# Third stage of a four-layer network: the order of all operations from one table of phases

## The chip, the cores and the metric

The kernel runs on one core of one Trainium2 chip. The metric is the device time of one execution in microseconds (us), as the median over runs of the same kernel. A core has a matrix engine (TensorE, PE in the profile; its weight loads are PEld), a vector engine (VectorE, DVE), a scalar engine (ScalarE, ACT), a general engine (GpSimd, POOL) and a sync engine whose queue (SP) issues transfers. Each engine takes its instructions in program order and waits for the others by semaphores.

## The reference, cut to what matters

The input x has shape (8192, 8, 16, 16). Four layers follow each other, each of the form x = x + layer(group norm(x)):

```
x = x + L0(gn(x))    # a tensor-train matrix of ranks 1, 8, 8, 1, plus a bias
x = x + L1(gn(x))    # 3x3 convolution, batch norm over all samples, ReLU
x = x + L2(gn(x))    # x and weights quantized to whole numbers by their global maxima,
                     # 3x3 convolution, divided by both scales, plus a bias
x = x + L3(gn(x))    # 3x3 convolution with edge padding, weights sign(w) * mean|w|, plus a bias
```

gn normalizes each sample over 4 groups of 2 channels. Two numbers need all samples before any sample can go on: the batch norm's moments (end of layer 1) and the maximum of |gn(x)| (start of layer 2's convolution). So the kernel has three stages; the third does layer 2's convolution, layer 3's group norm and layer 3's convolution.

## The kernel before

**Tiles.** The 8192 samples are 64 tiles of 128 samples. In the second and third stage a tile is an array of 128 partitions (8 channels x 16 rows) by 2048 columns (128 samples x 16 image columns), 1 MB. Thirteen tiles stay on the chip between the stages, the others are read from memory by `load3`, which is called at `rows2` for the tile four places on.

**What the third stage does with a tile.** It is cut into 26 operations, each a short function with a short name. In the order in which one tile goes through them:

- `rows2` (DVE), `spread2` (PE): the scale of each sample, from a small array spread over the partitions; it is written to columns 0 to 127 of the accumulator `ps_a` (read as `r2`).
- `v` (DVE, two halves, to int8), `q` (ACT, to bf16): quantized x. `bias` (ACT) adds layer 2's bias to the first half of x.
- `c2h0`, `c2h1` (PE, 6 products each, `pq` in the profile): layer 2's convolution of each half; `stz` (DVE) evicts the first half into x, `z1` (ACT) the second into a buffer that `add1` (POOL) adds to x.
- `sq` (ACT), `sums` (PE, 16 products, `s`), `small` (DVE, six short instructions), `pow` (POOL), `rows3` (DVE), `spread3` (PE, to `ps_r` and `ps_o`): layer 3's group statistics. `small` puts its transposed sums in columns 160 to 191 of `ps_a` (`st3`), and `rows3` reads them there.
- `t` (DVE, two halves): scaled x. `hi` (ACT): t rounded[...]; `lo` (POOL): the remainder; `edl` (ACT): the edge columns of lo (those of hi belong to `hi`). `c` (ACT) and `corr` (POOL): the offset of the group norm and the bias, added to x.
- `c3h0`, `c3h1` (PE, 12 products each, `pf`): layer 3's convolution of each half, six products with hi and six with lo; `out0`, `out1` (DVE) evict them into x. After the second, SP sends the tile to memory.

The four products of halves take turns in two accumulators of two banks each (`ps_c`): each one waits until the product before the last has been evicted.

**What sets the order.** Every engine's instructions keep the order in which the program names the operations. That order is the list `todo`. Its middle is written turn by turn from `TURN`, in which each operation has the offset of its tile: in a turn, `rows2` of tile i + 3 stands beside `out1` of tile i - 3, so a tile needs seven turns. The first 151 entries are replaced by `C_HEAD` and the last 130 by `C_TAIL`, two lists that name each operation with its tile (negative numbers count from the last tile: `spread2:-1` is tile 63). In `C_TAIL`, `small:-4` (tile 60) stands ahead of `spread2:-1`:

```
C_TAIL = """
...
bias:-2 t:-5 stz:-2 lo:-6 edl:-6 sums:-4 small:-4 bias:-3 corr:-6 c:-5 spread2:-1 c2h0:-3 stz:-3 pow:-4 c3h1:-7
...
```

For the last three tiles `c` is left out, and `corr` is done by DVE (two instructions) instead of POOL: see `offset3` and `add3`. Both convolution halves of layer 3 are one operation each, with the products of hi first, then those of lo: see `layer3`.

Of the kernel before, what the change touches and what calls it, by code (L numbers as in the profile page):

```python
# [8 lines left out]
F32 = mybir.dt.float32  # L9
# [4 lines left out]
ALU = mybir.AluOpType  # L14
# [4 lines left out]
P = 128  # L19
C, H, W = 8, 16, 16  # L20
# [5 lines left out]
QS = P // NQ  # L26
BANK = QS * W
# [17 lines left out]

C_HEAD = """
rows2:0 spread2:0 v:0 rows2:1 q:0 spread2:1 c2h1:0 rows2:2 bias:0 v:1 spread2:2 rows2:3 c2h0:0 v:2 z1:0 q:1
spread2:3 stz:0 add1:0 bias:1 c2h1:1 sq:0 c2h0:1 z1:1 v:3 sums:0 stz:1 small:0 q:2 add1:1 c2h0:2 c2h1:2 bias:2  # L50
rows2:4 pow:0 sq:1 rows2:5 rows3:0 z1:2 spread2:4 spread3:0 stz:2 t:0 q:3 sums:1 hi:0 c:0 small:1 v:4 add1:2 pow:1
bias:3 c2h0:3 spread2:5 rows3:1 sq:2 c2h1:3 spread3:1 stz:3 lo:0 sums:2 t:1 rows2:6 corr:0 edl:0 small:2 c:1 q:4
z1:3 hi:1 c3h0:0 pow:2 c3h1:0 v:5 add1:3 rows3:2 out0:0 bias:4 out1:0 lo:1 sq:3 q:5 spread3:2 spread2:6 c2h0:4 c:2
corr:1 edl:1 c2h1:4 rows2:7 z1:4 stz:4 t:2 hi:2 sums:3 c3h1:1 small:3 v:6 c3h0:1 out1:1 c2h1:5 pow:3 bias:5 rows3:3
spread3:3 lo:2 out0:1 q:6 spread2:7 rows2:8 z1:5 edl:2 v:7 c:3 add1:4 sq:4 c2h0:5 c3h0:2 bias:6 t:3 corr:2 stz:5
sums:4 c3h1:2 small:4 add1:5 hi:3 out0:2 c2h0:6 pow:4 rows3:4 sq:5 out1:2 spread2:8 stz:6 spread3:4 t:4 lo:3 c2h1:6
z1:6 corr:3 edl:3 sums:5 c:4 hi:4 small:5 pow:5 bias:7 v:8 q:7 add1:6
""".split()
C_TAIL = """
c2h1:-4 sq:-5 rows2:-2 rows3:-6 out1:-8 spread3:-6 rows2:-1 spread2:-2 c2h0:-4 v:-2 sums:-5 stz:-4 z1:-4 q:-3 t:-6  # L60
edl:-7 c3h0:-7 q:-2 small:-5 c2h1:-3 c:-6 out0:-7 c2h0:-2 hi:-6 add1:-4 sq:-4 pow:-5 rows3:-5 z1:-3 spread3:-5
bias:-2 t:-5 stz:-2 lo:-6 edl:-6 sums:-4 small:-4 bias:-3 corr:-6 c:-5 spread2:-1 c2h0:-3 stz:-3 pow:-4 c3h1:-7
hi:-5 out1:-7 c3h0:-6 rows3:-4 spread3:-4 add1:-3 c2h1:-2 sq:-3 lo:-5 z1:-2 out0:-6 v:-1 c3h1:-6 edl:-5 q:-1 add1:-2
sums:-3 t:-4 corr:-5 c:-4 c3h1:-5 out1:-6 small:-3 sq:-2 pow:-3 hi:-4 out1:-5 lo:-4 rows3:-3 bias:-1 sums:-2 c2h1:-1
small:-2 z1:-1 spread3:-3 edl:-4 c2h0:-1 c3h0:-5 c:-3 t:-3 stz:-1 add1:-1 pow:-2 corr:-3 rows3:-2 c3h1:-4 hi:-3
spread3:-2 sq:-1 out0:-5 c:-2 corr:-4 sums:-1 t:-2 lo:-3 hi:-2 small:-1 pow:-1 out1:-4 c3h0:-4 corr:-2 rows3:-1
out0:-4 edl:-3 c3h0:-3 spread3:-1 t:-1 lo:-2 c3h1:-3 out0:-3 edl:-2 out1:-3 hi:-1 c:-1 lo:-1 c3h0:-2 c3h1:-2 edl:-1
out0:-2 c3h0:-1 out1:-2 corr:-1 c3h1:-1 out0:-1 out1:-1
""".split()

# [6 lines left out]
def tile_net(ctx: ExitStack, tc: tile.TileContext, xb, xt_in, pack0, pack1, pack2, out):  # L79
    nc = tc.nc  # L80
    NT = xt_in.shape[0]

    pe, dve, act, pool = (InOrder(tc, e) for e in (nc.tensor, nc.vector, nc.scalar, nc.gpsimd))
# [78 lines left out]
    L = {}  # L162
# [127 lines left out]
    HALVES = [(0, P // 2), (P // 2, P)]  # L290

    def samples(t):
        return t.rearrange("p (b w) -> p b w", w=W)

    def over_w(stat, a, b):

        return stat[:, a:b].unsqueeze(2).to_broadcast([P, b - a, W])
# [25 lines left out]
    with first as s:  # L323
        small = s.enter_context(tc.tile_pool(name="small1", bufs=3))
# [5 lines left out]
        T = [dict() for _ in range(NT)]  # L330
# [267 lines left out]
        for n in range(NT * NQ):  # L598
            t, q = divmod(n, NQ)
# [62 lines left out]
        t = NT - 1  # L662
# [84 lines left out]
    small = ctx.enter_context(tc.tile_pool(name="small", bufs=4))  # L747
    kept = {}
    with tc.tile_pool(name="p2", bufs=2) as p2, tc.tile_pool(name="ps2", bufs=2, space=PSUM) as ps2:
        T = T2  # L750
# [8 lines left out]
        for k in range(3):  # L759
            nc.tensor.matmul(kps, L["gpad"].rearrange("p q j -> p (q j)"), L["band3"][:, k],  # L760
                             start=(k == 0), stop=(k == 2))
# [83 lines left out]
        for i in range(NT + 4):  # L845
# [4 lines left out]
            elif late:  # L850
                k, j = late.pop(0)
# [28 lines left out]
    with ExitStack() as s:  # L880
        wk = s.enter_context(tc.tile_pool(name="wk3", bufs=2))
        ps_c = s.enter_context(tc.tile_pool(name="ps_c3", bufs=2, space=PSUM))
# [4 lines left out]
        T = [dict() for _ in range(NT)]  # L887
# [4 lines left out]
        r2, r3, o3 = ps_a[:, 0:P], ps_r[:, 0:P], ps_o[:, 0:P]  # L892
# [11 lines left out]
        def halves(t):  # L904
            return t.rearrange("p (h n) -> p h n", h=2)
# [68 lines left out]
            stats_pow(T[i]["mv"])  # L974

        def offset3(i):
            if i >= NT - 3:
                return
            T[i]["c"] = small.tile([P, P], F32, name=f"c_{i}", tag="c")
            act.activation(T[i]["c"], o3, AF.Identity, bias=L["bias3"], scale=1.0)  # L980

# [20 lines left out]

        def add3(i):
            x = samples(T[i]["x"])
            if i >= NT - 3:
                for a, b in HALVES:
                    dve.scalar_tensor_tensor(x[:, a:b], over_w(o3, a, b), L["bias3"], x[:, a:b], ALU.add, ALU.add)
                return
            pool.tensor_tensor(x, x, over_w(T[i].pop("c"), 0, P), ALU.add)

        def edges3(i):
            edges(T[i]["lo"])

        def layer3(i, h):
            pc = ps_c.tile([P, 2, BANK], F32, name=f"pf_{i}_{h}", tag="pc")
            for m, t in enumerate(("hi", "lo")):
                for k in range(2):
                    q = 2 * h + k
                    tv = T[i][t][:, q * QS:(q + 1) * QS]
                    for n in range(3):  # L1020
                        pe.matmul(samples(pc[:, k]), L["sign3"][:, n], tv[:, :, n:n + W],
                                  start=(m == n == 0), stop=(m == 1 and n == 2))
            T[i]["pf", h] = pc

        def finish(i, h):
            x = halves(T[i]["x"])[:, h]
            pc = T[i].pop(("pf", h)).rearrange("p k n -> p (k n)")
            dve.scalar_tensor_tensor(x, pc, L["scale3"], x, ALU.mult, ALU.add)
            T[i]["done"] = T[i].get("done", 0) + 1
            if T[i]["done"] == 2:  # L1030
                nc.sync.dma_start(out[order[i]], T[i]["x"])
                T[i].clear()

        OPS = {"rows2": rows2, "spread2": spread2, "v": scale2, "q": round2, "bias": bias2,
               "c2h0": lambda i: layer2(i, 0), "stz": first2, "c2h1": lambda i: layer2(i, 1), "z1": second2, "add1": add2,
               "sq": square3, "sums": sums3, "small": stats3, "pow": pow3, "rows3": rows3, "spread3": spread3, "c": offset3,
               "t": scale3, "hi": high3, "lo": low3, "corr": add3, "edl": edges3,
               "c3h0": lambda i: layer3(i, 0), "out0": lambda i: finish(i, 0),
               "c3h1": lambda i: layer3(i, 1), "out1": lambda i: finish(i, 1)}
        TURN = [("rows2", 3), ("rows3", -1), ("out1", -3), ("sq", 0), ("c2h0", 1), ("stz", 1), ("spread2", 3), ("spread3", -1),  # L1040
                ("c", -1), ("c2h1", 1), ("z1", 1), ("add1", 1), ("v", 3), ("sums", 0), ("small", 0), ("pow", 0), ("t", -1),
                ("edl", -2), ("q", 2), ("hi", -1), ("bias", 2), ("lo", -1), ("corr", -1), ("c3h0", -2), ("out0", -2),
                ("c3h1", -2)]
        todo = [(op, i + k) for i in range(-3, NT + 4) for op, k in TURN if 0 <= i + k < NT]
        if len(todo) >= len(C_HEAD) + len(C_TAIL):
            head, tail = ([(op, int(i) + n) for op, i in (c.split(":") for c in l)] for l, n in ((C_HEAD, 0), (C_TAIL, NT)))
            todo = head + todo[len(head):len(todo) - len(tail)] + tail
        for i in range(AHEAD):
            load3(i)
        for op, i in todo:  # L1050
# [72 lines left out]
```

## Time and profile before

| what | us |
|---|---|
| median of 3 runs | 3834.26 (3833.98 to 3834.51) |
| span of the profiled execution | 3831.54 |
| time around the span, against the median | 2.7 |
| third stage: first DVE operation, end of last eviction | 3064.64, 3826.39 |
| PE busy over the span | 3606.5 (94%) |
| DVE | 3406.9 (89%) |
| POOL | 3040.9 (79%) |
| ACT | 2513.1 (66%) |
| groups of the third stage, one each: `v`, `t`, per half | 1.21 |
| `lo`, `corr`, `add1`, `pow` on POOL | 4.27, 3.69, 2.42, 1.02 |
| `hi`, `q`, `sq`, `z1`, `bias` on ACT | 1.93, 1.90, 1.90, 1.21, 1.15 |
| `stz`, `out0`, `out1` on DVE | 1.28, 1.26, 1.26 |

No time of the profiled execution beyond its span is recorded; 3831.54 is set beside the median, and the runs differ among themselves by 0.5. The page's busy shares are means over three stages of different make: the third is the last fifth of the span. In it all engines work on different tiles at once, so what counts is which engine is never idle, and who waits for whom where it is. Since a helper records every operation, all of them carry the same line (L43), and groups are told apart by the names of their tiles: x is `xs`, `u`, `xk`, `ys` or `bs`, t is `sq` or `xh`.

### The profile page before, as it was taken

The page shows a single profiled execution, that of the slowest core. Times are in us where ns is not written, and L with a number is a line of the kernel's source. Part 1 is how long each engine was busy: PE and PEld are TensorE (multiplying, and loading weights), DVE is VectorE, ACT ScalarE, POOL GpSimd, SP SyncE. Part 2 cuts the span into 40 slices and gives each one's busy share as a digit, 9 for nine tenths or more (in the row PEclk, how much of TensorE's full clock was granted, in tenths as well). Part 3 has the DMA queues.
Part 4 walks back from the last instruction along what each step waited for, and adds up shares of the span by engine and source line. Part 5 has one row for each costly group of instructions (what it writes and reads, how often), then busy time and mean ns, then how long its engine had stood idle before and what let it go on. Part 6 is the DMA issues. An engine that isn't in the chain of part 4 may idle for free. (4 is left out here: it accounts for less than half of the span.)

```text
span 3831.5 us, 52833 instructions
## 1 busy us (share of the span) xinstructions
PE 3606.5 (94%) x16326; PEld 2127.6 (56%) x16326; DVE 3406.9 (89%) x6319; ACT 2513.1 (66%) x2673; POOL 3040.9 (79%) x3101
## 2 busy tenths in 40 slices
PE   8999999999999999999999999997655599999998
PEld 4666666666666666666666666662211155555555
DVE  8988888888888888888888888877998889999997
ACT  5666666666666666666666666665665477777775
POOL 4877778777777787777777877766887779999997
PEclk9999999999999999999999999998776699999999
DMA  5787787888877878788788788757999724444432
GB/s 212 255 268 258 258 266 251 270 253 262 270 256 258 267 250 271 253 262 267 258 261 266 250 271 252 258 187 281 422 425 425 301 110 176 187 185 178 185 145 99
DMA packets 210809, 960.93 MB, mean 251 GB/s; under 512 B 44896, under 2 KB 45152, under 8 KB 110048
## 3 DMA queue, kind: packets, MB, share of 16 engines
q1 hardware_dynamic: 173808, 692.22, 48.7%
q0 software_dynamic: 36288, 264.26, 23.4%
q8 instruction: 131, 2.15, 0.2%
q14 instruction: 150, 1.23, 0.1%
q10 hardware_dynamic: 432, 1.08, 0.1%
HBM read 578.84 MB, written 378.54 MB: 250 GB/s over the span
## 5 line engine op out<-in xcount | busy, mean ns | idle before, releaser
L43 PE MATMUL po<-u,core 128*128 128x512 f32 (+1 forms) x4112 | 1844.7, 591 | 0.0
L43 ACT COPY u<-pu 128x2048 f32<-128x2048 f32 x512 | 956.7, 1868 | 511.9 <-PE pu L43 511.8
L43 PEld LDWEIGHTS po<-u,core 128*128 128x128 f32 x4112 | 744.7, 190 | 737.1 <-issue 736.1
L43 PE MATMUL pu<-core2r,xl 128*128 128x256 f32 x4032 | 678.5, 310 | 4.5 <-ACT u L43 3.6
L43 PEld LDWEIGHTS pu<-core2r,xl 128*128 128x128 f32 x4032 | 527.9, 189 | 127.8 <-issue 123.0
L43 POOL TENSOR_TENSOR bs<-bs,xh 128x512 fp32r<-128x512 f32 (+1 forms) x253 | 325.6, 1287 | 201.0 <-ACT xh L43 200.9
L43 POOL TENSOR_TENSOR v<-e 128x128 f32<-128x128 f32 x750 | 397.9, 542 | 0.0
L43 DVE TENSOR_TENSOR xs<-po,xs 128x512 f32<-128x512 f32 x256 | 177.0, 692 | 217.5 <-PE po L43 217.5
L43 ACT ACTIVATE m<-pm,b 128x128 f32<-128x128 f32 x250 | 92.0, 368 | 395.5 <-PE pm L43 395.5
L43 PEld LDWEIGHTS pm<-v,fast 128*128 128x128 f32 x2000 | 262.5, 191 | 119.7 <-issue 106.2
L43 POOL TENSOR_TENSOR e<-x1n,x 128x512 f32<-128x512 f32 x250 | 306.2, 1225 | 23.9 <-ACT x L43 16.4
L43 DVE TENSOR_TENSOR bs<-bs,stat 128x1024 f32<-128x1024 f32 x252 | 290.8, 1217 | 2.1
L43 POOL TENSOR_TENSOR xs<-xs,w 128x2048 f32<-128x2048 f32 x64 | 291.5, 4554 | 0.6 <-DMA xs<-in_xt 0.6
L43 PE MATMUL pm<-v,fast 128*128 128x128 f32 x2000 | 263.6, 275 | 0.0
L43 ACT ACTIVATE x<-x1n 128x512 f32<-128x512 f32 x500 | 247.1, 545 | 7.6 <-DVE x1n L43 7.6
L43 POOL TENSOR_TENSOR mv<-mv,mhalf 128x4 f32<-128x4 f32 x127 | 130.8, 1030 | 138.1 <-DVE mv L43 138.1
L43 PE MATMUL pf<-hi,sign 128*128 128x512 f32 x768 | 227.7, 434 | 0.5 <-DVE xs L43 0.5
L43 POOL DMA_DIRECT2D xl<-limb_d x252 | 150.0, 595 | 96.9 <-ACT x L43 29.1
L43 PE MATMUL pf<-lo,sign 128*128 128x512 f32 x768 | 219.4, 423 | 0.0
L43 POOL TENSOR_TENSOR v<-r 128x128 f32<-128x128 f32 x500 | 215.9, 448 | 0.0
L43 ACT ACTIVATE sq<-xs 128x2048 f32<-128x2048 f32 x103 | 196.8, 1911 | 4.7 <-POOL xs L43 4.6
L43 PE MATMUL gb<-rows_c,sel 128*128 128x128 f32 x128 | 40.3, 409 | 167.3 <-DVE rows_c L43 167.3
(310 smaller groups left out, 7202.4 us busy)
## 6 DMA issues: line engine op xcount, KB each, us to landing
xl<-limb_d POOLq DMA_DIRECT2D x252, 1024.0 KB, 7.4
x_d<-xs SPq DMA_DIRECT2D x76, 1024.0 KB, 8.4
xs<-in_xt SPq DMA_DIRECT2D x64, 1024.0 KB, 7.5
bs<-in_xb SPq DMA_DIRECT2D x63, 1024.0 KB, 5.7
limb_d<-xh SPq DMA_DIRECT2D x1008, 64.0 KB, 4.3
limb_d<-bs SPq DMA_DIRECT2D x1008, 64.0 KB, 5.2
y_d<-ys SPq DMA_DIRECT2D x60, 1024.0 KB, 8.0
u<-x_d SPq DMA_DIRECT2D x34, 1024.0 KB, 5.9
```

Source lines behind the costliest of these rows:

```text
L43: return self.tc.keep_in_program_order(op(*args, **kwargs))
```

## The change

The two lists and `TURN` go. In their place stands a table that gives each operation a phase, and a period; all operations of all tiles are sorted by period times tile plus phase, from the first to the last, with nothing special at the ends. The phases are only keys of the sort: no instruction waits for a time. Each half of layer 3's convolution is named as two operations, a (hi) and b (lo), which have phases of their own; a takes the accumulator. The exceptions of `offset3` and `add3` for the last three tiles are removed. Up to the third stage the program is the same, instruction by instruction.

```diff
-C_HEAD = """
-rows2:0 spread2:0 v:0 rows2:1 q:0 spread2:1 c2h1:0 rows2:2 bias:0 v:1 spread2:2 rows2:3 c2h0:0 v:2 z1:0 q:1
...
-C_TAIL = """
...
+PERIOD = 11.539
+PHASE = {"rows2": 0, "spread2": 0.01, "v": 5.1, "q": 10.2, "bias": 10.4, "c2h1": 11.6, "z1": 13.1, "c2h0": 16.1, "add1": 17.1,
+         "stz": 23.1, "sq": 24, "sums": 31.8, "small": 34.7, "pow": 37.3, "rows3": 42.7, "spread3": 45.3, "t": 46.3,
+         "hi": 49.9, "c": 51.2, "lo": 51.9, "corr": 58.8, "edl": 60.3, "c3h0a": 60.4, "c3h0b": 61.3, "out0": 66.8,
+         "c3h1a": 69.3, "c3h1b": 69.4, "out1": 69.41}
...
         def offset3(i):
-            if i >= NT - 3:
-                return
             T[i]["c"] = small.tile([P, P], F32, name=f"c_{i}", tag="c")
...
         def add3(i):
             x = samples(T[i]["x"])
-            if i >= NT - 3:
-                for a, b in HALVES:
-                    dve.scalar_tensor_tensor(x[:, a:b], over_w(o3, a, b), L["bias3"], x[:, a:b], ALU.add, ALU.add)
-                return
             pool.tensor_tensor(x, x, over_w(T[i].pop("c"), 0, P), ALU.add)
...
-        def layer3(i, h):
-            pc = ps_c.tile([P, 2, BANK], F32, name=f"pf_{i}_{h}", tag="pc")
-            for m, t in enumerate(("hi", "lo")):
-                for k in range(2):
...
+        def layer3(i, h, m):
+            if m == 0:
+                T[i]["pf", h] = ps_c.tile([P, 2, BANK], F32, name=f"pf_{i}_{h}", tag="pc")
+            pc, t = T[i]["pf", h], T[i]["hi" if m == 0 else "lo"]
+            for k in range(2):
...
-        TURN = [("rows2", 3), ("rows3", -1), ("out1", -3), ("sq", 0), ("c2h0", 1), ("stz", 1), ("spread2", 3), ("spread3", -1),
-                ("c", -1), ("c2h1", 1), ("z1", 1), ("add1", 1), ("v", 3), ("sums", 0), ("small", 0), ("pow", 0), ("t", -1),
-                ("edl", -2), ("q", 2), ("hi", -1), ("bias", 2), ("lo", -1), ("corr", -1), ("c3h0", -2), ("out0", -2),
-                ("c3h1", -2)]
-        todo = [(op, i + k) for i in range(-3, NT + 4) for op, k in TURN if 0 <= i + k < NT]
...
+        todo = [(op, i) for _, op, i in sorted((PERIOD * i + at, op, i) for op, at in PHASE.items() for i in range(NT))]
```

Sorted, the steady turn of the new order reads, with the tile of each operation counted from the newest (0), engine by engine:

| engine | before | after |
|---|---|---|
| PE | c2h0 -2, spread2 0, spread3 -4, c2h1 -2, sums -3, c3h0 -5, c3h1 -5 | spread2 0, c2h1 -1, c3h1 -6, c3h0 -5, c2h0 -1, sums -2, spread3 -3 |
| DVE | rows2 0, rows3 -4, out1 -6, stz -2, v 0, small -3, t -4, out0 -5 | rows2 0, stz -2, small -3, t -4, out1 -6, v 0, rows3 -3, out0 -5 |
| ACT | sq -3, c -4, z1 -2, edl -5, q -1, hi -4, bias -1 | sq -2, z1 -1, edl -5, hi -4, c -4, q 0, bias 0 |
| POOL | add1 -2, pow -3, lo -4, corr -4 | corr -5, pow -3, add1 -1, lo -4 |

The order of PE in the table of before is that of one turn as the program names it; the chain of a turn may be begun at any of its entries.

More of the change, by code (lines that the diff above doesn't have):

```diff
@@ L44, in __getattr__ @@
         return call
-C_HEAD = """
-rows2:0 spread2:0 v:0 rows2:1 q:0 spread2:1 c2h1:0 rows2:2 bias:0 v:1 spread2:2 rows2:3 c2h0:0 v:2 z1:0 q:1
[L50 to L58, printed above, removed]
-C_TAIL = """
-c2h1:-4 sq:-5 rows2:-2 rows3:-6 out1:-8 spread3:-6 rows2:-1 spread2:-2 c2h0:-4 v:-2 sums:-5 stz:-4 z1:-4 q:-3 t:-6
@@ L61 @@
[L61 to L69, printed above, removed]
+PERIOD = 11.539
[3 more added lines that the diff above has]
+         "c3h1a": 69.3, "c3h1b": 69.4, "out1": 69.41}
@@ L1012, in edges3 @@
             edges(T[i]["lo"])
-        def layer3(i, h):
-            pc = ps_c.tile([P, 2, BANK], F32, name=f"pf_{i}_{h}", tag="pc")
-            for m, t in enumerate(("hi", "lo")):
-                for k in range(2):
[L1018 to L1023, printed above, removed]
+        def layer3(i, h, m):
[3 more added lines that the diff above has]
+            for k in range(2):
+                q = 2 * h + k
+                tv = t[:, q * QS:(q + 1) * QS]
+                for n in range(3):
+                    pe.matmul(samples(pc[:, k]), L["sign3"][:, n], tv[:, :, n:n + W],
+                              start=(m == n == 0), stop=(m == 1 and n == 2))
         def finish(i, h):
@@ L1037, in tile_net @@
                "t": scale3, "hi": high3, "lo": low3, "corr": add3, "edl": edges3,
-               "c3h0": lambda i: layer3(i, 0), "out0": lambda i: finish(i, 0),
-               "c3h1": lambda i: layer3(i, 1), "out1": lambda i: finish(i, 1)}
-        TURN = [("rows2", 3), ("rows3", -1), ("out1", -3), ("sq", 0), ("c2h0", 1), ("stz", 1), ("spread2", 3), ("spread3", -1),
-                ("c", -1), ("c2h1", 1), ("z1", 1), ("add1", 1), ("v", 3), ("sums", 0), ("small", 0), ("pow", 0), ("t", -1),
-                ("edl", -2), ("q", 2), ("hi", -1), ("bias", 2), ("lo", -1), ("corr", -1), ("c3h0", -2), ("out0", -2),
-                ("c3h1", -2)]
-        todo = [(op, i + k) for i in range(-3, NT + 4) for op, k in TURN if 0 <= i + k < NT]
-        if len(todo) >= len(C_HEAD) + len(C_TAIL):
-            head, tail = ([(op, int(i) + n) for op, i in (c.split(":") for c in l)] for l, n in ((C_HEAD, 0), (C_TAIL, NT)))
-            todo = head + todo[len(head):len(todo) - len(tail)] + tail
+               "c3h0a": lambda i: layer3(i, 0, 0), "c3h0b": lambda i: layer3(i, 0, 1), "out0": lambda i: finish(i, 0),
+               "c3h1a": lambda i: layer3(i, 1, 0), "c3h1b": lambda i: layer3(i, 1, 1), "out1": lambda i: finish(i, 1)}
+        todo = [(op, i) for _, op, i in sorted((PERIOD * i + at, op, i) for op, at in PHASE.items() for i in range(NT))]
         for i in range(AHEAD):
```

## The prediction

> **What bounds the kernel now.** The change begins where the third stage begins, so I read that stage alone. First the table of stretches: the steady middle (first row) and the end.
>
> ```profile
> core 0: us, PE busy (x) PEld busy (x) DVE busy (x) ACT busy (x) POOL busy (x), PEclk, DMA share, GB/s
> 3400.00:3500.00 100.00, 100.00 (x500) 59.08 (x499) 93.27 (x165) 77.47 (x69) 97.51 (x36) 1.00 0.47 181
> ...
> 3760.00:3780.00 20.00, 16.14 (x75) 9.34 (x73) 12.49 (x26) 11.98 (x12) 17.42 (x7) 0.91 0.13 52
> 3780.00:3800.00 20.00, 20.00 (x104) 11.78 (x106) 18.00 (x33) 15.01 (x13) 18.34 (x8) 1.00 0.13 54
> ```
>
> In the middle TensorE (PE) is never idle, but POOL (97.5%) and DVE (93%) have little to spare; near 3770 PE has idled and its clock dropped. Then the chain of waits, which in the middle is PE alone:
>
> ```profile
> 3398.32 6.42 PE pf L43 x24
> ...
> 3744.71 6.42 PE pf L43 x24
> ```
>
> Thirty turns in 346.39 us: **11.546 us a turn**, one tile entering and one leaving. Then the timeline of PE, one steady turn from layer 2's products (pq) to the next turn's:
>
> ```profile
> 3404.57 1.47 PE L43 MATMUL pq<-q,band 128*128 128x512 bf16 x6
> 3405.88 0.39 PE L43 MATMUL ps_a<-rows_d,sel 128*128 128x128 f32 x2
> 3406.10 0.39 PE L43 MATMUL ps_r<-rows_e,sel 128*128 128x128 f32 x2
> ...
> 3409.79 1.82 PE L43 MATMUL pf<-hi,sign 128*128 128x512 f32 x6
> 3411.45 1.71 PE L43 MATMUL pf<-lo,sign 128*128 128x512 f32 x6
> 3413.00 1.72 PE L43 MATMUL pf<-hi,sign 128*128 128x512 f32 x6
> 3414.57 1.71 PE L43 MATMUL pf<-lo,sign 128*128 128x512 f32 x6
> ```
>
> Starts follow each other without a hole, so the turn is the sum of the starts' distances. Last, the waits and the timeline at the end:
>
> ```profile
> PE ps_a L43 <- DVE mv L43: 3.0, 1, 3.0
> PE pq L43 <- DVE bs L43: 0.8, 1, 0.8
> PE pf L43 <- DVE xs L43: 0.5, 2, 0.3
> ...
> POOL lo L43 <- ACT hi L43: 6.0, 3, 3.6
> ```
>
> ```profile
> 3764.45 1.04 PE L43 MATMUL s<-sq,wsum 128*32 128x512 f32 x8
> 3768.51 0.80 PE L43 MATMUL ps_a<-rows_d,sel 128*128 128x128 f32 x2 [3.02 <-DVE mv L43]
> 3769.10 2.72 PE L43 MATMUL pq<-q,band 128*128 128x512 bf16 x6
> ```
>
> PE waited 3.0 us for DVE, and the next six pq products took 2.72 us instead of 1.47.
>
> **The whole stage as an account of PE.** From DVE's first operation (3064.64) to the end of the last eviction (3826.39) are 761.75 us; 64 turns of work are 738.9. The other 22.9: waits in the head 10.2 (distances of starts beyond the usual ones: 0.7, 3.2, 1.1, 0.8, 1.2, 0.6, 2.6, 0.1), slow clock in the head about 4.5, the tail 6.8 (waits 1.0, 3.1, 0.45 and 0.33; slow clock 1.9), and 1.5 for the last product's end and its eviction. That adds to 23.0. A new order can change only the turn, the head and the tail.
>
> [...]spread2 writes columns 0 to 127 of ps_a, small reads columns 160 on, and PE still waited for the last read (mv).[...]
>
> **Part 1, the two groups.** In the table c3h0a and c3h0b (and c3h1a and c3h1b) have no other PE operation between their places, for any tile; the order of PE has high and low of a half next to each other everywhere. The accumulator is taken at the same place. Cost and gain: nothing.
>
> **Part 2, the steady turn.** No operation is added or dropped. PE's order per turn was c2h0, spread2, spread3, c2h1, sums, c3h0, c3h1; it becomes c2h1, c3h1 (older tile), c3h0, c2h0, sums, spread3, spread2. So two joins go (pq to spread; sums to pf) and two come (sums to spread; pq to pf). Sums to pf delays the first group: 3409.79 to 3411.45 is 1.66, a group inside 1.56, so 0.10 goes. Sums to a spread with no wait isn't in the trace; a spread after a wait is: 3076.47 to the following pq at 3076.80 is 0.33 against 0.22, so 0.11 comes. If that were hidden it would be 0[...]. Pq to pf is in the head: 3117.78 to 3120.62 is 2.84, against 1.31 + 1.56 = 2.87. The turn becomes 11.546 - 0.01, with bounds -0.13 and +0.10; over some 58 turns **-0.6 us** (-7.5 to +6).
>
> Will PE still never wait? I walked one turn with the measured durations (v and t 2.34 each, evictions 1.2 to 1.3, small 1.46, rows3 0.8; ACT hi 1.93, sq 1.90, z1 1.21, q 1.90; POOL lo 4.27, corr 3.69, add1 2.42, pow 1.02). The inputs that come closest: spread2 after rows2, 0.6 us early; c3h1 after stz frees its accumulator, 1.0; c3h0 after z1 frees the other, 1.0; c2h1 after q, 1.3; c2h0 after out1, 1.5; spread3 after rows3, 1.7; low products after edl, 2.1. (The second, from spread3 at 0: spread2 at 0.55, c2h1 at 0.78, so c3h1 at 2.1; stz, behind out0 and rows2 on DVE, ended at 1.0.) DVE, with 10.8 us of work, now idles 0.8 before out1, which stands behind t and waits for PE; v and rows3 queue behind it, and q on ACT waits for v: that is in the 1.3. POOL needs 4.23 + 3.65 + 2.37 + 1.02 = 11.27 from start to start; its waits (lo for hi, add1 for z1) fill the other 0.27. PE covers all this.
>
> Transfers: the tile's output leaves SP after out1, the same six turns after rows2 as now, and the load into its buffer 4 us later (out at 3406.15, load at 3410.18), landing in 6 to 9 us; it is read seven turns, 81 us, after. SP has no other queue here, POOL issues none: no cost.
>
> **Part 3, the head.** The table fills one tile per turn, the old list let layer 2 run ahead and put c3h0:0 and c3h1:0 side by side. Out1:0 comes some 6 us later, but that is not a loss: PE does other tiles meanwhile. Its waits, walked with the same durations: 0.6 and 3.0 (rows2:0, rows2:1 behind v:0 on DVE) and 0.9 (q:0), as now; 1.8, 0.9, 0.4 and 1.4 for q:1 to q:4, and 1.6 for rows3:1: **10.6 against 10.2**. One of them in full, from the stage's first operation: v:1 runs on DVE from 5.1 to 7.5; ACT takes z1:0 first (8.0 to 9.2, behind c2h1:0 at half clock) and then q:1 (9.1 to 11.0); PE is through with c2h0:0 and spread2:2 at 9.3, so c2h1:1 waits from 9.3 to 11.1, the 1.8. The slow clock I take as equal; it is 1 us either way. Part 3: +0.4 (-2 to +3).
>
> **Part 4, the tail.** The old list moved spread2:63 behind small:60 on ps_a; small:60 stood on DVE behind t:58 (3763.45, 2.35) and stz:61 (3765.72, 1.28), and ended at 3768.45. In the table spread2:63 keeps its steady place, 0.6 us behind rows2:63, and c2h0:62 no longer waits for out0. So the waits 1.0 + 3.1 + 0.45 + 0.33 and the 1.9 of slow clock go: 6.8. What is late next: when no new tiles enter, PE's turn shrinks to spread3 plus pf, 6.7 us, and POOL's lo + corr to 7.9. Corr of the last three tiles returns from DVE (2.47 each) to POOL (3.69), with c on ACT (0.36). POOL had idled 6.0 us before lo in the tail, so only corr:62, between lo:62 and lo:63, delays: PE, some 3 us behind, waits 0.4 us for edl:63 and 0.3 for rows3:63. Part 4: **-6.8 + 0.7 = -6.1** (-8 to -2).
>
> **Sum.** -0.6 + 0.4 - 6.1 = -6.3. The walk as a whole, laid against the trace of before, was 0.35 us short there; its own difference is -6.6, and -7 with the shorter turn; I take -6.7. The profiled span 3831.54 becomes 3824.8. The median 3834.26 is 2.7 above that span: 3827.6 us. 0.2%, about what a measurement of this kernel can tell from no change, is 7.7 us, down to 3826.6: the forecast lies just short of it.
>
> **The rivals.**
> A, faster: the first spread after sums is hidden. Then 0.11 x 58 = 6.4 more go: 3821.2. For it: weights of pf are loaded under the product before. Against: the same load after sums showed 0.10.
> B, no gain: the head costs what the tail gives, the 6 us of out1:0 surviving to the end: 3834. For it: POOL, at 97.5%, cannot catch up a late start quickly. Against: PE's waits, not out1:0, make the account.
> C, slower: POOL becomes the bound. Its 11.27 is 0.27 under PE's turn. If lo waits for hi and add1 for z1 one after the other, 0.5 us in all, the turn is 11.8: 60 x 0.25 - 6 = +9, 3843. It is slower by over 0.2% from 11.78 on. For it: add1 now stands between pow and lo, and z1 behind sq on ACT. Against: the walk has 0.31 of such waits, with 2 us between lo and the product that needs it.
> That the groups change nothing is Part 1, not a rival.
>
> **Numbers.** Main case 0.62 (3825 to 3831), A 0.18, B 0.13, C 0.07. A third of the main case lies beyond 3826.6, which with A makes faster 0.38; same 0.55 from the rest of it and B; slower 0.07. The range 3822.5 to 3832 leaves out C, the far part of A and the upper half of B.
>
> **What would show it.** Steady PE chain 11.53 to 11.55 a turn; out1:0 about 47 us after the stage's first operation; no wait of ps_a for mv, clock 1.00 from 3740 on; the last out1 near 3819.7. Wrong if the turn is over 11.6 with PE waiting for lo or q, or if the tail has a PE wait over 2 us.

## The result, and the profile after

| what | before | after |
|---|---|---|
| median, us (11 runs each) | 3832.91 (3831.44 to 3834.51) | 3824.30 (3822.28 to 3825.91) |
| ratio, 95% interval | | 0.9977 (0.9968 to 0.9986) |
| span of the profiled execution | 3831.54 | 3822.81 |
| third stage, first DVE operation to end of last eviction | 761.75 | 752.57 |
| steady turn | 11.546 | 11.473 |

The change takes 8.6 us off, 0.23%; the forecast was that it takes off 6.7. All of it is in the third stage: that stage is 9.18 us shorter and starts 0.4 us later in the profiled execution.

The table of stretches of the kernel after (columns as before): the steady middle first, then the end.

```profile
core 0: us, PE busy (x) PEld busy (x) DVE busy (x) ACT busy (x) POOL busy (x), PEclk, DMA share, GB/s
3400.00:3500.00 100.00, 99.53 (x502) 58.35 (x510) 92.26 (x170) 79.25 (x71) 98.36 (x35) 1.00 0.49 188
3760.00:3780.00 20.00, 19.95 (x102) 12.31 (x94) 17.52 (x34) 16.59 (x16) 19.81 (x9) 1.00 0.15 63
3780.00:3800.00 20.00, 19.64 (x99) 11.72 (x99) 15.59 (x30) 8.38 (x9) 18.17 (x7) 1.00 0.32 131
```

From 3760 to 3780 PE is busy for 19.95 us instead of 16.14, and its clock is 1.00 instead of 0.91. The shares of the middle look like those of before, although the turn there is shorter: a busy share doesn't show that. The chain of waits does (start, duration, what):

```profile
3384.47 6.15 PE pf L43 x24
...
3728.66 6.15 PE pf L43 x24
```

Thirty turns in 344.19 us: 11.473 a turn. In PE's timeline of one turn the starts tell where it went:

```profile
3486.27 1.46 PE L43 MATMUL pq<-q,band 128*128 128x512 bf16 x6
3487.37 1.90 PE L43 MATMUL pf<-hi,sign 128*128 128x512 f32 x6
3489.11 1.70 PE L43 MATMUL pf<-lo,sign 128*128 128x512 f32 x6
3490.64 1.70 PE L43 MATMUL pf<-hi,sign 128*128 128x512 f32 x6
3492.17 1.70 PE L43 MATMUL pf<-lo,sign 128*128 128x512 f32 x6
3493.71 1.47 PE L43 MATMUL pq<-q,band 128*128 128x512 bf16 x5
```

The last three groups of six start 1.53, 1.53 and 1.54 us apart; before, they were 1.55, 1.57 and (from 3414.57 to the next product) 1.55 apart. All 24 products are closer together. Instruction by instruction, the mean distance of starts inside such a row of 24 is 0.2558 us here and 0.2590 before. I call these the **256 pace** and the **259 pace**.

The waits of PE in the tail, from 3740 on, are down to two small ones (total us, count, longest; counted as distances of starts beyond the usual ones, as in the account below, they come to 0.51 and 0.47):

```profile
PE pf L43 <- ACT lo L43: 0.3, 1, 0.3
PE ps_r L43 <- DVE rows_e L43: 0.3, 1, 0.3
```

The account of the stage, made as for the kernel before (waits are distances of starts beyond the usual ones; slow clock in the head is what is left over, with the few rows of 24 at the ends that have the 259 pace):

| us | before | after |
|---|---|---|
| 64 turns | 738.9 | 734.3 |
| waits in the head | 10.2 | 10.1 |
| slow clock in the head, and rest | 4.5 | 5.7 |
| waits in the tail | 4.9 | 1.0 |
| slow clock in the tail | 1.9 | 0 |
| end of the last product and its eviction | 1.5 | 1.5 |
| sum | 761.9 | 752.6 |

So in this execution the tail brought 5.8 us, the turn 4.6, and the head took 1.1.

### The profile page after: what moved, and what is told of

Same layout as the page of the kernel before. It is cut to its first block, busy times and chain, and to the rows that moved or that the text cites. A ratio compares the mean times of both kernels' runs of the same rounds, so it can differ in the third digit from the quotient of the medians.

```text
span 3822.8 us, 52777 instructions
## 1 busy us (share of the span) xinstructions
PE 3598.8 (94%) x16264; PEld 2127.1 (56%) x16326; DVE 3386.0 (89%) x6313; ACT 2518.2 (66%) x2676; POOL 3048.8 (80%) x3104
## 4 chain that ended last, share of the span: by engine, by line
PE 85%; DVE 6%; DMA 4%; issue 2%; POOL 1%; ACT 1%; POOLq 0%; SPq 0%; DVEq 0%; ACTq 0%
PE po L43 45%; PE pu L43 12%; PE pf L43 10%; PE pm L43 6%; PE pq L43 4%; PE s L43 3%; PE pc L43 3%; DVE top L43 3%; PE ps_r L43 1%; DMA ys<-x_d 1%; DMA x_d<-u 1%; DMA x_d<-ys 1%; DMA u<-x_d 1%; DMA x_d<-xs 1%; DMA sq<-y_d 1%
```

## The experiments

Two questions. Do head, turn and tail have the shares of this account? And why are layer 3's products closer together: what stands ahead of them on PE, or what other engines do beside them?

**The head alone.**

```diff
+            table = [(op, i) for _, op, i in sorted((PERIOD * i + at, op, i) for op, at in PHASE.items() for i in range(NT))]
+            first = table[:255]
+            todo = first + [o for o in todo if o not in first]
```

> The kernel before with the first 255 operations taken from the table and the rest in the old order (layer 3's halves unsplit, the exception for the last three tiles kept). It measures the head by itself. As predicted (Part 3): +0.4 us against before, and some 0.6 us where the two orders meet (two waits of layer 2's products by the measured durations), so +1.0, bounds -1.5 to +3.5. By the account of the trace after, in which the head has about 1.1 us more of waits and slow clock, less some six turns of 0.07 us: +1.3. A head that costs all of its late start (rival B): +6.

Measured: 3834.33 us (13 runs), 1.0003 of before (0.9995 to 1.0011), which is +1.2 with an interval from -1.9 to +4.2. From PE's first spread to the last eviction the profiled execution has 760.94 us, before 761.09. The table's head costs about nothing, although out1:0 comes 6 us later; that the account has 1.1 for it is one execution's figure. In the kernel after, profiled a second time, the eviction of the first half of tile 10 began 0.95 us sooner (153.08 us after the first spread, not 154.03), and that stage was 1.0 shorter. The order is the same; what differs is that PE ran at half clock for one stretch of 3.41 us in the head, and in the first execution for 6.83. Rival B, in which that delay lives on to the end, is out.

**Head and turns from the table, the tail old.**

```diff
-            first = table[:255]
+            first = table[:-264]
```

> The kernel before with all but the last 264 operations taken from the table, and these last ones in the old order. Head and steady turns are the table's, the tail is the old one. Against head_only it differs in some 43 steady turns. Prediction (turn shorter by 0.01): 0.4 us below head_only, no gain against before. Rival, the turn gives near half of what the change brings (0.073 a turn as in the trace after): 3.1 us below head_only, some 2 us below before. If so, what is missing to the change, about 6 to 7 us, is the tail.

Measured: 3830.14 us (13 runs), 0.9993 of before (0.9985 to 1.0001), 4.2 us below the run with the new head alone; the expectation from the measured turn was 3.1, from the prediction 0.4. The turn is 11.473. By the profiled executions, which differ by 4.0 us in the stage, the rest lies in the clock: PE waits here as long as before for the last read of ps_a, but the clock stays at 1.00. Timeline; then the two stretches of 3.41 us that hold the wait, and for comparison those of the kernel before:

```profile
3766.53 0.49 PE L43 MATMUL ps_a<-rows_d,sel 128*128 128x128 f32 x2 [3.01 <-DVE mv L43]
3766.85 1.46 PE L43 MATMUL pq<-q,band 128*128 128x512 bf16 x6
```

```profile
3761.61:3765.02 3.41, 1.91 (x17) 0.40 (x16) 3.41 (x4) 2.88 (x4) 3.41 (x2) 1.00 0.00 0
3765.02:3768.43 3.41, 1.91 (x10) 1.21 (x11) 1.32 (x7) 1.04 (x2) 3.41 (x2) 1.00 0.00 0
```

```profile
3764.81:3768.22 3.41, 0.68 (x8) 0.00 (x0) 3.31 (x6) 2.72 (x4) 3.41 (x2) 1.00 0.00 0
3768.22:3771.64 3.42, 3.13 (x9) 1.63 (x9) 0.20 (x2) 0.00 (x0) 3.42 (x3) 0.50 0.00 0
```

The six products after the wait take 1.46 us, not 2.72. The stretches are not chosen freely: in each of the eleven traces all changes of the granted clock (913 in all) lie whole multiples of 3.413 us apart, to within 10 ns, and the stretches here begin and end at such multiples. In the kernel before, 2.73 us of the wait lie in one of them, in which PE is busy for 0.68 us, and the next runs at half clock; so it is in the run with the head alone (0.66). Here the end of a stretch cuts the same wait into 1.50 and 1.51, PE is busy for 1.91 us in each, and the clock stays at 1.00. Counted over all eleven traces: of 9704 such stretches at full clock, the 375 in which PE was busy for less than 1.40 us were all followed by one at half clock, 68 of the 76 with 1.40 to 1.65 us, and of the 9253 with more than 1.65 us none. So the same wait went with 1.9 us of slow clock in the kernel before and with none here; where it fell among the stretches differs. No trace shows why the clock falls.

From PE's first spread to the last eviction this run has 756.90 us, and the kernel after 751.91: the tail is the difference, 5.0 in these two executions (this one had lost nothing to the clock there) and 5.8 by the medians. The runs of a kernel spread by 3 us, so the two figures are not told apart.

**One operation of the old tail moved.**

```diff
-... sums:-4 small:-4 bias:-3 corr:-6 c:-5 spread2:-1 c2h0:-3 ...
+... sums:-4 spread2:-1 small:-4 bias:-3 corr:-6 c:-5 c2h0:-3 ...
```

> The kernel before with one edit: spread2 of the last tile is moved ahead of small of tile 60, no other operation is moved. The wait of 3.0 us of PE for ps_a goes, and the slow clock that followed it. Theory of the tail (Part 4): -3.1 - 1.9 = -5.0, with -4 as the end where some of it comes back as a later wait; turn unchanged at 11.546. Rival: what PE gains it loses again at the next operand that is late (hi, lo or an accumulator), change under 1 us.

Measured: 3829.14 us (21 runs), 0.9989 of before (0.9983 to 0.9996): 4.0 us less, and the turn stays at 11.547. PE's timeline at the place, and the stretch:

```profile
3766.40 1.04 PE L43 MATMUL s<-sq,wsum 128*32 128x512 f32 x8
3767.37 0.49 PE L43 MATMUL ps_a<-rows_d,sel 128*128 128x128 f32 x2
3767.70 1.46 PE L43 MATMUL pq<-q,band 128*128 128x512 bf16 x6
```

```profile
3760.00:3780.00 20.00, 19.05 (x90) 11.46 (x90) 16.75 (x31) 15.63 (x16) 20.00 (x9) 1.00 0.13 52
```

The spread follows sums with no wait and the clock stays up. So one operation, put behind a reader of other columns of `ps_a` (160 to 191; it writes 0 to 127) and kept waiting for it for 3.02 us, was most of the old tail's loss. What it leaves are the waits of 0.8 for an accumulator and of 0.7 ahead of pf, which the table doesn't have.

**Sums back ahead of layer 3's products.**

```diff
-PHASE = {... "v": 5.1, ... "sums": 31.8, "small": 34.7, ... "out0": 66.8, ... "out1": 69.41}
+PHASE = {... "v": 2, ... "sums": 34.68, "small": 34.9, ... "out0": 69.25, ... "out1": 77.7}
```

> The kernel after with sums moved from behind c2h0 to directly ahead of c3h1 (phases of sums, small, v, out0 and out1 changed so that nothing waits in the steady turn): PE's turn is spread2, c2h1, sums, c3h1, c3h0, c2h0, spread3, so layer 3's products follow sums again, as before, and no longer a product of layer 2. If what stands ahead of the 24 products sets their pace: distance of starts 0.259 instead of 0.2558, turn 11.55. If it is something else in the new order (which engine works beside them, or where): 0.2558 and a turn of 11.48. Head and tail are longer here than in the kernel after, by about 11.6 us by the measured durations (a tile needs longer for its way), so the time is near 3836 (turn 11.48) or 3840 (11.55); the turn decides, not the time.

Measured: 3847.87 us (5 runs), 1.0042 of before (1.0030 to 1.0055); turn 11.67. The time is longer than the 3836 or 3840 expected since the walk missed a wait in each turn: ahead of the second half, PE waits for the accumulator that z1 frees. Timeline:

```profile
3400.14 1.82 PE L43 MATMUL pf<-hi,sign 128*128 128x512 f32 x6
3401.81 1.71 PE L43 MATMUL pf<-lo,sign 128*128 128x512 f32 x6
3403.39 1.82 PE L43 MATMUL pf<-hi,sign 128*128 128x512 f32 x6
3405.05 1.71 PE L43 MATMUL pf<-lo,sign 128*128 128x512 f32 x6
```

The first group of each half takes 1.67 and 1.66 us to the next start, the second 1.58 and 1.56, so the 0.10 called a shown weight load comes twice. (Read from the kernel before, behind sums: a load of 0.19 us begins within 2 ns of the first product, and the second product starts 0.367 us after the first, not 0.260.) That accounts for the turn: 11.473 + 0.04 of wait + 0.10 for the second shown load + 0.06 for the pace, 11.67. Inside the rows the mean distance without these joins is 0.2583, and the median 0.258 to 0.259. The pace is that of before, with the new order around it. That speaks for what stands ahead, though with the wait it isn't a clean run.

**A spread ahead of layer 3's products.**

```diff
-PHASE = {"rows2": 0, "spread2": 0.01, ...
+PHASE = {"rows2": 0, "spread2": 0.063, ...
```

> The kernel after with one number changed: the phase of spread2, 0.01, becomes 0.063. PE's turn is c2h1, spread2, c3h1, c3h0, c2h0, sums, spread3: layer 3's products follow a spread with no wait, and no longer a product of layer 2; all other engines keep their order. If only a start behind sums (whose first weight load is not hidden) sets the slow pace: distance of starts 0.2558 as in after, turn 11.473. If it takes a product of layer 2 ahead of them: 0.259, turn 11.55. The head is longer, by 5.2 us by the measured durations (spread2 comes later for the first tiles), so about 3830 or 3834; the turn decides.

Measured: 3833.46 us (13 runs), 0.9999 of before (0.9991 to 1.0007); turn 11.540. All of it that differs from the kernel after in the steady turn is one spread's place on PE. The chain of waits:

```profile
3391.86 6.21 PE pf L43 x24
3403.40 6.21 PE pf L43 x24
```

No engine keeps PE waiting in the middle, and each row of 24 has the 259 pace (0.2588), 6.21 instead of 6.15. So it isn't a shown weight load that brings the 259 pace, since here the load is hidden: from the start of the spread's two products to the start of the second group are 1.77 us (3506.87 to 3508.64), and the two products take 0.22 and a group 1.56. The stage is 9.4 us longer than in the kernel after: 6.2 of it by the time that tile 10 is evicted (the head), and the rest at 0.067 a turn.

**Sums between the spreads and layer 2's product.** A spread behind sums shows 0.10 us of its first weight load (0.213 us to the next start in the kernel after, not 0.112); a product of layer 2 should show only 0.01, as in the one place in the kernel before (0.227, not 0.216).

```diff
-PHASE = {... "v": 5.1, ... "sums": 31.8, "small": 34.7, ... "out0": 66.8, ... "out1": 69.41}
+PHASE = {... "v": 2, ... "sums": 34.647, "small": 34.917, ... "out0": 69.25, ... "out1": 76.73}
```

> The kernel after with sums between spread2 and c2h1 (phases: sums 34.647, small 34.917, v 2, out0 69.25, out1 76.73): PE's turn is spread3, spread2, sums, c2h1, c3h1, c3h0, c2h0. A spread behind sums shows 0.10 us of its first weight load (0.213 to the next start, not 0.112); a product of layer 2 behind sums showed 0.01 (0.227, not 0.216) in the kernel before. So the turn should lose 0.09: 11.38 if layer 3's products keep the pace of 0.2558 behind c2h1, 11.46 if sums one step further ahead brings back 0.259. Over some 58 turns -5 or -1 us, and about -0.5 at the ends by the measured durations: 3818.5 against 3824.3 of after, or 3823. Rival: POOL, whose four operations take 11.27 from start to start, becomes the bound with its waits for hi and z1: turn 11.5 to 11.6, no gain.

Measured: 3821.58 us (5 runs), 0.9968 of before (0.9956 to 0.9981); turn 11.410. The chain of waits:

```profile
3394.96 6.15 PE pf L43 x24
3406.34 6.20 PE pf L43 x24
3417.78 6.15 PE pf L43 x24
3429.16 6.20 PE pf L43 x24
```

The first distance behind sums is 0.525 and the next 0.226, against 0.523 and 0.213 (with a usual distance of 0.216 and 0.112) for a spread: the 0.09 a turn came. But the pace now goes to and fro, one turn at 256 and one at 259, and half of its gain is lost: 11.41 is the mean of 11.38 and 11.44. POOL is busy for 98.84 of 100 us and does not bound: PE has no wait in the middle.

**The two spreads swapped, and the kernel after beside it.**

```diff
-PHASE = {"rows2": 0, "spread2": 0.01, ...
+PHASE = {"rows2": -1.0, "spread2": -0.9, ...
```

> The kernel sums_between with rows2 and spread2 at -1.0 and -0.9: on PE spread2 then stands ahead of spread3 instead of behind it, all else keeps its order, and the sum of PE's durations is the same. In sums_between the pace of layer 3's products went to and fro from turn to turn (0.2557, 0.2587). If the pace hangs on what PE itself did just before (or on which buffer is read), this order gives the same: 11.41 a turn, 3821.6. If it hangs on finer timing than the order of PE's instructions, it may lock on one of the two: 11.375 (some 2 us less, 3819.5) or 11.445 (3823.5). Ends as in sums_between, within 0.4 us by the measured durations.

> The kernel after, unchanged, beside the one with the spreads swapped: 0.9977 of before (0.9968 to 0.9986); it tells whether the shorter turn of sums_between is a gain over after on one chip (11.41 against 11.473 a turn, some 3 us).

Measured: 3821.87 us (5 runs), 0.9967 of before (0.9954 to 0.9979), turn 11.410; the kernel after 3823.98 (10 runs), 0.9975 (0.9966 to 0.9984), turn 11.473. The pace alternates again. With sums moved alone, the rows at 256 fall in the turns in which DVE writes t to the array named xh; with the spreads swapped as well, in those with sq. So which buffer is read doesn't decide. Nor do the neighbours seem to: by the median, from one kind of row to the other, the instructions of DVE and ACT that run at its start have begun within 2 ns of the same distance, POOL's within 50 ns. On this chip all five runs with the spreads swapped are faster than all ten of the kernel after (3819.06 to 3822.66 against 3823.22 to 3825.48), so the shorter turn is a gain of some 2 us.

**Corr of the last three tiles back on DVE** (the exceptions of `offset3` and `add3` put back into the kernel after).

```diff
+            if i >= NT - 3:
+                return
...
+            if i >= NT - 3:
+                for a, b in HALVES:
+                    dve.scalar_tensor_tensor(x[:, a:b], over_w(o3, a, b), L["bias3"], x[:, a:b], ALU.add, ALU.add)
+                return
```

> The kernel after with the exception for the last three tiles put back: c left out, corr by DVE in two instructions. It is the price of the return of corr to POOL. Prediction (Part 4): the return brought the two late waits of 0.4 and 0.3 us of the tail, so the exception gives at most -0.7. Walk of the whole tail with measured durations: +0.9, since DVE, with 2.47 us more for each tile, evicts later (rows3 of tile 63 then waits 1.7). Both within 1 us of after, near 3825.

Measured: 3824.33 us (12 runs), 0.9977 of before (0.9968 to 0.9986): no difference to after that can be told. The profile says why. The wait for edl:63 is gone, but spread3 of the last tile waits longer:

```profile
3799.27 0.49 PE L43 MATMUL ps_r<-rows_e,sel 128*128 128x128 f32 x2 [1.45 <-DVE rows_e L43]
```

**What the traces say together on the pace.** A row of 24 products of layer 3 that stands alone and has no wait inside it, in the eleven traces of these kernels, sorted by what PE does right before it (by the mean of its distances after the first, under or over 0.257; the last row of the table is the first 24 of the 60 products that end the kernel, behind the last spread3, in the six traces where no wait lies in them):

| ahead of the row | rows | at the 256 pace |
|---|---|---|
| sums | 172 | 3 |
| a spread | 66 | 0 |
| a product of layer 2 | 362 | 292 |
| the last spread3 | 6 | 4 |

The last row is the exception to the second. In the kernel after it reads:

```profile
3799.91 0.39 PE L43 MATMUL ps_o<-rows_e,corr 128*128 128x128 f32 x2
3800.05 1.78 PE L43 MATMUL pf<-hi,sign 128*128 128x512 f32 x6
3801.67 1.70 PE L43 MATMUL pf<-lo,sign 128*128 128x512 f32 x6
3803.20 1.70 PE L43 MATMUL pf<-hi,sign 128*128 128x512 f32 x6
```

From 3801.67 on, the groups of six start 1.53 apart, behind a spread. In three of the four such cases the spread itself had waited 0.3 us for its input; in the fourth, with the spreads swapped, PE had not waited. So what stands ahead goes with the pace in the steady turn, but it is no rule without exception.

The make of the row alone doesn't set the pace: in the new order it begins with the second half of the older tile, in the old order both halves are of one tile; but the kernels with sums or a spread ahead have the new make and the 259 pace.

A row keeps its pace from its first products to its last while the other engines change operations several times: over its first seven distances, the next seven and the last eight the mean is 0.2591, 0.2590 and 0.2589 before (58 rows), and 0.2562, 0.2557 and 0.2554 in the 57 rows of the kernel after that have the 256 pace. Each cycle of it runs: a product starts, the next weight load starts, it takes 0.191, and the next product starts. The first gap is 3.1 ns before and 4.9 ns after, the last 65.0 and 60.3: nearly the whole difference lies on PE between the loads and the products. That loads and products set the spacing together is not shown: layer 2's products, with loads of 0.098, are 0.216 apart at 480 columns and 0.217 at 512, and they differ from layer 3's in the type of their data too.

Shown: in the steady turn, what stands ahead of the row on PE changes its pace (one spread moved, the order on all other engines kept). That the other engines have no part in it is argued from the even pace inside the rows, not shown. Open: why two rows behind the same operation differ, as in the two kernels with sums moved. The start differs with the pace (first distance behind layer 2 0.450 for 256, 0.441 or 0.442 for 259, in nearly all rows), so it is settled there, but not by anything that the trace shows.

## Why the prediction was right, point by point

The direction and the three places were right, and one term was mis-sized. The measured 3824.30 lies in the range (3822.5 to 3832), but below the main case's 3825 to 3831, about midway between the forecast and rival A's 3821.2. The forecast, 3827.6, was 3.3 too high: 2.0 of it is the span (3824.8 against 3822.81: 2.5 from the stage, less 0.4 for its later start), and 1.2 that the median lies 1.5 above its span and not 2.7. The 2.7 set one execution's span beside the median of three others, which was 1.35 above that of all eleven; in each of the later runs of before and after the time is 1.7 or 1.8 above that run's own span.

Part of the hit is luck. The turn gave 4.0 us more than its term, head and tail together 1.0 less than theirs, the 6.7 taken for parts that add to 6.3 brought the total 0.4 nearer, and the bound that held the turn was set for another cause. Of the signs named, the turn of 11.53 to 11.55 and the last out1 near 3819.7 did not come (11.473 and 3817.6).

- **What bounds it: right.** PE is never kept waiting for data in the middle of the kernel after; the order of waits held, and DVE and POOL stay under PE's turn. Rival C is out: even a turn of 11.41, with sums moved, is not bounded by POOL's 11.27.
- **Part 1, the groups: nothing**, as said; high and low stand next to each other in every row of 24 in the trace.
- **Part 2, the turn: this step failed.** It was put at -0.01 and is -0.073 a turn; the bound of -0.13, set for a hidden spread, held it (that of +0.10 was the author's estimate, 0.2 in place of 0.11, and is not shown). The joins were right, each of them: the first spread after sums is not hidden (0.213 instead of 0.112, where 0.11 more was taken), the shown load ahead of pf goes (0.107), and the first product behind pq costs what it did in the head, to within 0.01. So rival A's mechanism, a hidden spread, did not come. The mis-sized term is the products themselves: a join was priced by its own distances, and the 22 distances behind it were taken as given, but they went from 0.2590 to 0.2558, which is 0.072 of the 0.073. The head of the kernel before had shown a row of 12 behind pq, but at the 259 pace, so that instance said nothing against it.
- **Part 3, the head: +0.4, measured +1.1 by the account**, inside its bounds, and about nothing by the run with the head alone. The waits are 10.1 against 10.6 (the eight listed for the kernel before add to 10.3, not 10.2): for q:1 to q:4 0.92, 0.87, 0.42 and 1.24 (taken as 1.8, 0.9, 0.4 and 1.4), for rows3:1 1.77 (1.6). What is more is slow clock, which was taken as equal with 1 us either way, and that is its size: around two waits that follow each other the clock is at half for 6.83 us in this execution, and for 3.41 in the second execution of the same kernel. PE's timeline there, and the table of stretches (the clock is the number behind POOL's), follow this list. Out1:0 ends 48.4 us after the stage's first operation (47.5 in the second execution, 47 forecast), and costs nothing by itself.
- **Part 4, the tail: -6.1, measured -5.8.** The waits that go and the clock that returns are those named, and what is late next is what was named: edl:63 (0.51) and rows3:63 (0.47), where 0.4 and 0.3 were taken. Its charge for the return of corr was only half the story: corr on POOL does delay edl:63, but on DVE it delays rows3:63 by more (1.45 us of wait). Of the slow clock: in the stretch of 3.41 us ahead of it PE was not wholly idle, but busy for 0.68 us. And of the wait: PE stood 3.02 us for `mv`, a read of columns of `ps_a` that the spread doesn't write; by what means it is held there, no trace shows.
- **Wrong would have been** a turn over 11.6 or a wait of PE over 2 us in the tail; neither is there.

```profile
3094.52 0.49 PE L43 MATMUL ps_r<-rows_e,sel 128*128 128x128 f32 x2 [1.71 <-DVE diag_d L43]
...
3096.58 1.44 PE L43 MATMUL pq<-q,band 128*128 128x512 bf16 x3 [1.07 <-ACT q L43]
```

```profile
3095.00:3100.00 5.00, 3.70 (x13) 2.06 (x13) 4.79 (x9) 5.00 (x4) 5.00 (x2) 0.57 0.00 0
3100.00:3105.00 5.00, 5.00 (x21) 3.05 (x20) 3.57 (x8) 4.97 (x6) 5.00 (x3) 0.75 0.00 0
```

Two waits, 1.71 and 1.07, with 1.0 us of work between them, and the clock is at 0.57 and 0.75 of its full rate in the ten microseconds that hold or follow them. In the second execution of the same kernel it is at 0.66 and 1.00 in the same two stretches.

## What to carry to other kernels

On an engine that is never idle the price of a join is not only its own gap: measure the distances of all instructions behind it, in both orders, since a row of equal products ran at two paces here, 0.2558 and 0.2590 us a product. In the tail of a pipeline look for an operation that stands behind a reader of its accumulator without need: here one wait of 3.02 us, and 4.0 us for moving one entry of a list. An order from one table can be changed by one number, which makes such places cheap to try: with sums moved between the spreads and layer 2's product the kernel takes 3821.58 us, 0.9968 of before (0.9956 to 0.9981); its turn is 0.063 us shorter than that of the kernel after. The intervals of the two against before still overlap; beside the kernel after on one chip it was run only with the spreads swapped, and there all its runs were faster.

## What the runs showed of the hardware that was not expected

- Rows of the same 24 products with 128x128 fp32 weights ran at two paces, 0.2558 and 0.2590 us a product, and kept the one they started with (0.2562 over the first seven distances and 0.2554 over the last eight, in the 57 rows of the kernel after at the first pace; 0.2591 and 0.2589 before).
- Behind sums (32-column products) the first distance of 128x128 fp32 products was 0.10 us longer than usual (0.213 instead of 0.112 for a spread, 0.367 instead of 0.260 for layer 3), that of 128x128 bf16 ones 0.01 (0.226 and 0.227 instead of 0.216).
- All 913 changes of PE's granted clock in the eleven traces lie multiples of 3.413 us apart, to within 10 ns in each trace. Of the stretches of that length at full clock, those in which PE was busy, by the profile, for under 1.40 us were followed by half clock in all 375 cases, those over 1.65 us in none of 9253. A wait of 3.0 us was followed by half clock in two executions (0.68 and 0.66 us busy) and left it at 1.00 in a third, in which the end of a stretch cut the wait in half (1.91 and 1.91).
